# Rotating queries and keys: a shuffle on VectorE, or two DMAs between even and odd partitions

## The chip, the core and the metric

The kernel runs on one core of one Trainium2 chip. The metric is the device time of one execution in microseconds (us). Of the kernel before, three runs are at hand, with the median 1198.29 us (1196.13 to 1202.39), and one execution with a profile. The core has five engines that each work through their own list of instructions in order: TensorE (PE in the profile; its weight loads, PEld, are shown apart), VectorE (DVE), ScalarE (ACT), GpSimd (POOL) and SyncE (SP), which here only issues DMAs. ACT and POOL can issue DMAs too.

## What is computed

The input x holds 8 sequences of 512 tokens with 512 features. After a LayerNorm, a branch of linear attention (s) and a mixture of experts (g) are multiplied and added to x:

```python
xn = _layernorm(x)
q = silu((xn @ Wq).reshape(b, n, 16, 32));  k = silu((xn @ Wk).reshape(b, n, 16, 32))
q = _lrpe_rotate(q);  k = _lrpe_rotate(k)
o = _lightning_attn(q, k, v, log_lam)      # chunks of 128 tokens, decay by head
s = _gated_group_rmsnorm(o, xn @ Wg1 @ Wg2, norm_weight) @ Wo
g = silu(moe(xn))                          # top 4 of 16 experts, and a shared one
out = x + s * g

def _lrpe_rotate(x):                       # the last axis is one head, d = 32
    x1, x2 = x[..., :16], x[..., 16:]
    return concatenate([x1 * cos - x2 * sin, x1 * sin + x2 * cos], axis=-1)
```

So a feature i of a head, below 16, is rotated together with feature i + 16 of the same head, by an angle that depends on i and on the token. Scores are products of a rotated query with a rotated key over the 32 features of a head; they don't change if the features of both are put in another order.

## The kernel before, in words

Queries and keys are held with features on the partitions and the 512 tokens of a sequence along the free axis. The 16 heads lie in 4 groups (g) of 4 heads, so a group fills the 128 partitions, 32 for each head. Everything is float32. The weights and tables are prepared on the host (from L1310 on) and in `shape_constants`.

The work has four stages (times from the profiled execution):

1. 0 to about 200 us: norm, transpose, routing and the shared expert of all 8 sequences, with the attention of sequence 0 woven in.
2. About 200 to 330 us: the attention of sequence 1, beside the table of which token goes to which expert, and the first loads of expert weights (768 KB each).
3. About 330 to 735 us: 136 blocks of 128 tokens through their experts (gather on POOL, transpose by DMA, two matrix products).
4. About 735 to 1192 us: the attention of sequences 2 to 7, woven with `mixture`, which fetches for each tile of 128 tokens the rows m (shared expert, L1194) and s (attention of sequences 0 and 1, L1198) through SP and four rows yg of the experts (L1203) by indirect DMAs of POOL, adds them up on POOL and DVE, and multiplies and adds into xo (x itself, loaded at L1229; DVE at L1240, POOL at L1244, stored at L1245).

`rotated` makes one group of keys or queries. Four matmuls (L627, each in the profile's count two: four steps over the 512 features of the input, float32) put it into a PSUM bank; ACT takes it out with a silu into s (L632); DVE makes w_ from s by a `stream_shuffle` that exchanges the halves of 16 in each block of 32 partitions (L634, the list SWAP); then DVE multiplies s with the cosines into r (L636), w_ with the signed sines (L637), and adds (L638). s and w_ are taken from a ring of four buffers ("tmp"), which the attention's other short-lived tiles share (g1, rs, so). r is kT or qT of the group, two buffers each.

Who needs them: `by_token` transposes kT on PE (L654) and DVE multiplies it with the decay of its chunk (kd, L657); `scores` forms states from kd and v (L674), multiplies kT with qT in 4 banks (ps, L685), and DVE makes the scan of the states (L689), qd from qT (L705) and sc from ps with the decay mask (L711, four for a group). `output` (L722, L733) adds up po from both, and DVE multiplies it with the gate (L737). At the end of a sequence come the norm (`squares`, `normed`, L764, L769) and the projection with Wo (pw, L776).

The order on PE is written out by hand: `enter` (for sequence 2) begins with key 0, query 0, key 1, the transposes of key 0, query 1; `sequence` then takes for each group g its scores, key g+2, the transposes of group g+1, query g+2, and the output of group g, with projections of the sequence before between; groups 0 and 1 of the next sequence are made at its end. `last_sequence` does the same for sequence 7. Calls of `step` move the mixture of other tiles on. PSUM banks are scarce: four with the tag "a" (scores and others), one "k" (the transposes and states), one "m" (pk of `rotated`), two "d" (pq, po, pw). On the other engines a scheduler fixes the order, from each instruction's place in the program and the marks `behind(engine)`. SP issues all loads and stores except two loads of expert weights, which ACT issues (L1040), and the gathers, which POOL issues.

Of the kernel before, what the change touches and what calls it, by code (L numbers as in the profile page):

```python
# [20 lines left out]
B, N, D = 8, 512, 512  # L21
H, HD = 16, 32
G, HG = 4, 4
# [22 lines left out]
GROUP = 16  # L46


SWAP = [(i + HD // 2) % HD for i in range(HD)]


def shape_constants():

    f = np.float32
    c = {}
    lam = -(f(2.0) ** (f(-8.0) * (np.arange(H, dtype=f) + f(1.0)) / f(H))).astype(f)
    i = np.arange(C, dtype=f)
    diff = i[None, :] - i[:, None]
    dec = np.exp(lam[None, :, None] * np.maximum(diff, f(0.0))[:, None, :])
    c["dmask"] = np.where(diff[:, None, :] >= 0, dec, f(0.0))  # L60
    dq = np.exp(lam[:, None] * (i[None, :] + f(1.0)))
    c["dq"] = np.repeat(dq.reshape(G, HG, 1, C), HD, axis=2).reshape(G, P, C).transpose(1, 0, 2)
    c["dk"] = np.exp(lam[None, :] * (f(C) - f(1.0) - i[:, None]))
    lc = np.exp(lam * f(C))
    c["lamc"] = np.repeat(lc.reshape(G, HG, 1), HD, axis=2).reshape(G, P).T

    c["carry"] = np.tile(c["lamc"][:, :, None, None] * (np.arange(NC - 1) > 0), (1, 1, HD, 1))
    half = HD // 2
    theta = (f(BASE) ** (f(-2.0) * np.arange(half, dtype=f) / f(HD))).astype(f)
    ang = (np.arange(N, dtype=f)[None, :] * theta[:, None]).astype(f)  # L70
    c["cos"] = np.tile(np.cos(ang), (2 * HG, 1))
    c["sin"] = np.tile(np.concatenate([-np.sin(ang), np.sin(ang)], axis=0), (HG, 1))
    c["ident"] = np.eye(P)


    sel = np.zeros((P, H - HG + Q))
    exp = np.zeros((H, G, P))
    for g in range(G):
        for j in range(HG):
            sel[j * HD : (j + 1) * HD, H - HG + j] = 1.0 / HD  # L80
            exp[g * HG + j, g, j * HD : (j + 1) * HD] = 1.0
    c["sel"] = sel

    c["tri"] = np.triu(np.ones((P, P)), 1)
    c["iota_e"] = np.tile(np.arange(E), (P, 1))
    c["reset"] = np.tile((np.arange(NT) > 0)[None], (P, E)).reshape(P, E * NT)
    out = {k: np.ascontiguousarray(v.reshape(P, -1), dtype=f) for k, v in c.items()}
    out["exp"] = exp.reshape(H, D).astype(f)
    out["iota_b"] = (np.arange(P, dtype=f)[:, None] // Q * NBQ + np.arange(NBQ, dtype=f)).astype(f)
    out["token"] = (  # L90
        np.arange(NT)[None, :] * P + np.arange(P)[:, None] - B * N // 2).astype(np.float32)
    return out
# [3 lines left out]
def tile_block(ctx: ExitStack, tc: tile.TileContext, a: dict, out: bass.AP):  # L96
    nc = tc.nc
    PSUM = bass.MemoryType.PSUM
    x = a["x"]
# [5 lines left out]
    def bank(tag, name):  # L105
        return pp.tile([P, 512], F32, tag=tag, name=name, bufs={"a": 4, "k": 1, "m": 1, "d": 2}[tag])
# [10 lines left out]
    def load(pool, name, shape, dt=F32):  # L117
        t = pool.tile(shape, dt, tag=name, name=name, bufs=1)
        flat = t if len(shape) == 2 else t.rearrange(
            "p a b -> p (a b)" if len(shape) == 3 else "p a b c -> p (a b c)")  # L120
        nc.sync.dma_start(flat, a[name])
        return t

    def load_w(pool, name):
        t = pool.tile([P, KC, D], F32, tag=name, name=name, bufs=1)
        nc.sync.dma_start(t, a[name].rearrange("(k p) n -> p k n", p=P))
        return t
# [40 lines left out]
    wv = load_w(const, "wv")  # L168
# [6 lines left out]
    wk = load_w(const, "wk")  # L175
    cos = load(const, "cos", [P, N])
    sin = load(const, "sin", [P, N])
    wq = load_w(const, "wq")
# [23 lines left out]
    @contextmanager  # L202
    def on_pe():

        with tc.issue_after(last_pe[-1]) if last_pe else nullcontext():
            yield
        traced = nc.cur_bb.bb.instructions
        last_pe.append(next(
            i for i in reversed(traced) if i.engine == mybir.EngineType.PE))
# [413 lines left out]
    def rotated(b, g, n, w):  # L623
        ps = bank("m" if n == "k" else "d", f"p{n}_{b}_{g}")
        for k in range(KC):
            with on_pe():
                nc.tensor.matmul(  # L627
                    ps, lhsT=w[:, k, g * P : (g + 1) * P], rhs=xT_of[b][:, k, :],
                    start=(k == 0), stop=(k == KC - 1))
            between[0]()  # L630
        s = att.tile([P, N], F32, tag="tmp", name=f"s{n}_{b}_{g}", bufs=TMP)
        nc.scalar.activation(s, ps, AF.Silu)  # L632
        w_ = att.tile([P, N], F32, tag="tmp", name=f"sw{n}_{b}_{g}", bufs=TMP)
        nc.vector.stream_shuffle(w_, s, SWAP)  # L634
        r = att.tile([P, N], F32, tag=f"{n}T", name=f"{n}T_{b}_{g}", bufs=2)
        nc.vector.tensor_tensor(r, s, cos, ALU.mult)  # L636
        nc.vector.tensor_tensor(w_, w_, sin, ALU.mult)  # L637
        nc.vector.tensor_tensor(r, r, w_, ALU.add)  # L638
        return r

    def key(b, g):
        kT_of[g] = rotated(b, g, "k", wk)

    def query(b, g):
        qT_of[g] = rotated(b, g, "q", wq)
# [705 lines left out]
```

## Time and profile before

| | |
|---|---|
| median of three runs | 1198.29 us |
| the profiled execution | 1193.77 us |
| its span in the profile | 1191.9 us |
| mean granted TensorE clock | 0.991 |
| ACT busy | 459.7 us (39%), 934 instructions |
| POOL busy | 452.2 us (38%), 432 instructions |
| DMA, mean | 182 GB/s, 217.42 MB |
| the cos-multiply of L636, kT and qT | 732 and 869 ns |
| the sin-multiply of L637, swk and swq | 814 and 725 ns |
| the addition of L638, kT and qT | 772 and 945 ns |
| the silu of L632, sk and sq | 598 and 600 ns |
| the shuffle's list (L634 LOAD_MASK_SELECT) | some 10 ns |

The profile gives for each group of instructions the line of the code, the engine, the operation, the tile written and the tile read, the shape, the count, the busy time, the mean of one in ns, and the idle time of the engine just before them with what released it. "pk<-xT,wk" is a matmul that writes pk. The span is 1.9 us shorter than the execution's time. [...] An entry with SPq is the issue of a DMA on SP's queue, and its length is that of issuing, not of the transfer.

### The profile page before, as it was taken

To read this page: it belongs to the slowest core of one execution; us is meant where nothing else is said; L and a number is where in the kernel's file an instruction comes from. 1 tells how busy PE (TensorE), PEld (TensorE's weight loads), DVE (VectorE), ACT (ScalarE), POOL (GpSimd) and SP (SyncE) were. 2 spreads that over 40 slices of the span, in tenths; PEclk is the share of its full clock that TensorE was granted. 3 is DMA by queue.
4 is the path that set the end of the run, shared out by engine and by line. 5 is a ranking of instruction groups with operands and counts; after the bars stand their busy time and mean duration, and the time that the engine had idled before them with its cause. 6 is when DMAs were issued, how large, how long until landed. Compare 5 with 4: busy or idle time off the path is not lost. (4 is left out here: it accounts for less than half of the span.)

```text
span 1191.9 us, 21613 instructions
## 1 busy us (share of the span) xinstructions
PE 1145.7 (96%) x7780; PEld 700.9 (59%) x7780; DVE 722.8 (61%) x1557; ACT 459.7 (39%) x934; POOL 452.2 (38%) x432
## 2 busy tenths in 40 slices
PE   7999999989999999999999999999999989999997
PEld 3445554456577777677777775555554645545553
DVE  6356754889124444344444444969979598698684
ACT  4444454144374444444444442251251422422531
POOL 3211203200213333233333331762886848858211
PEclk9998999989999999999999999999999999999999
DMA  9964341191659999899999895931845637534112
GB/s 340 327 236 173 120 168 44 41 377 38 183 160 224 226 227 221 217 232 232 221 227 229 229 226 181 336 120 51 277 133 184 200 95 235 163 115 144 36 35 73
DMA packets 163499, 217.42 MB, mean 182 GB/s; under 512 B 89536, under 2 KB 98880, under 8 KB 161472
## 3 DMA queue, kind: packets, MB, share of 16 engines
q1 hardware_dynamic: 141984, 144.10, 40.5%
q0 software_dynamic: 21120, 70.34, 21.4%
q8 instruction: 65, 1.06, 0.4%
q10 hardware_dynamic: 288, 1.57, 0.4%
q14 instruction: 42, 0.34, 0.1%
HBM read 125.71 MB, written 72.42 MB: 166 GB/s over the span
## 5 line engine op out<-in xcount | busy, mean ns | idle before, releaser
L1103 PE MATMUL pgu<-wexp,xt 128*128 x1088 | 257.8, 380 | 3.2 <-ACT xt L1084 2.7
L1103 PEld LDWEIGHTS pgu<-wexp,xt 128*128 128x128 f32 x1088 | 205.8, 190 | 90.9 <-issue 39.2
L1062 POOL DMA_INDIRECT xg<-xn_d,slot x79 | 75.1, 951 | 243.4 <-DVE y L1133 159.2
L1108 DVE TENSOR_TENSOR slb<-slb,pgu 128x128 f32<-128x128 f32 x136 | 39.2, 288 | 196.7 <-ACT slb L1107 142.0
L1203 POOL DMA_INDIRECT yg<-y_d,place x128 | 143.0, 1117 | 34.6 <-issue 18.6
L1086 ACT COPY xt<-pl 128x512 uint16<-128x512 uint16 x136 | 104.3, 767 | 134.1 <-DMA pl<-xg 77.5
L1124 PE MATMUL py<-wexp,hT 128*128 x272 | 139.3, 594 | 0.1
L583 PE MATMUL pv<-wv,xT 128*128 128x512 f32 x256 | 119.4, 602 | 3.5 <-ACT sh L372 2.3
L627 PE MATMUL pk<-xT,wk 128*128 128x512 f32 x256 | 118.2, 603 | 1.7 <-DVEq L1167 1.7
L627 PE MATMUL pq<-xT,wq 128*128 128x512 f32 x256 | 117.3, 599 | 0.0
L776 PE MATMUL pw<-wo,on 128*128 128x512 f32 x224 | 103.8, 612 | 5.8 <-DVE m L1240 5.2
L1244 POOL TENSOR_TENSOR xo<-xo,m 128x512 f32<-128x512 f32 x31 | 45.1, 1454 | 141.3 <-DVE m L1240 133.4
L1062 POOL DMA_INDIRECT more<-xn_d,slot x57 | 54.0, 947 | 109.9 <-DVE y L1133 109.0
L711 DVE TENSOR_TENSOR sc<-ps,dmask 128x512 f32<-128x512 f32 x128 | 79.5, 680 | 5.6 <-remote 3.8
L627 PEld LDWEIGHTS pq<-xT,wq 128*128 128x128 f32 x256 | 47.8, 193 | 52.8 <-issue 51.3
L627 PEld LDWEIGHTS pk<-xT,wk 128*128 128x128 f32 x256 | 46.1, 190 | 52.0 <-issue 49.6
L1133 DVE TENSOR_SCALAR y<-py,xg 128x512 f32<-128x512 f32 x79 | 59.3, 750 | 28.2 <-PE py L1124 27.7
L776 PEld LDWEIGHTS pw<-wo,on 128*128 128x128 f32 x224 | 42.5, 196 | 56.9 <-issue 47.8
L583 PEld LDWEIGHTS pv<-wv,xT 128*128 128x128 f32 x256 | 45.7, 191 | 49.6 <-issue 43.5
L1107 ACT ACTIVATE slb<-pgu 128x128 f32<-128x128 f32 x136 | 37.8, 278 | 87.5 <-PE pgu L1103 83.1
L694 ACT COPY blocked<-state 32x96 f32<-32x96 f32 x96 | 30.7, 320 | 81.6 <-DVE state L689 68.8
L1133 DVE TENSOR_SCALAR y<-py,more 128x512 f32<-128x512 f32 x57 | 42.7, 750 | 19.7 <-PE py L1124 19.6
(172 smaller groups left out, 1761.5 us busy)
## 6 DMA issues: line engine op xcount, KB each, us to landing
y_d<-y SPq DMA_DIRECT2D x136, 256.0 KB
wexp<-in_experts SPq DMA_DIRECT2D x14, 768.0 KB
sh_d<-sh SPq DMA_DIRECT2D x32, 256.0 KB
m<-sh_d SPq DMA_DIRECT2D x32, 256.0 KB
xo<-in_x SPq DMA_DIRECT2D x32, 256.0 KB
out<-xo SPq DMA_DIRECT2D x31, 256.0 KB
x<-in_x SPq DMA_DIRECT2D x7, 1024.0 KB
xT_d<-xT SPq DMA_DIRECT2D x7, 1024.0 KB
```

Of the source, the lines that this page charges most:

```text
L583: nc.tensor.matmul(pv, lhsT=xT_of[b][:, k, t * P : (t + 1) * P], rhs=wv[:, k, :], start=(k == 0), stop=(k == KC - 1))
L627: nc.tensor.matmul(ps, lhsT=w[:, k, g * P : (g + 1) * P], rhs=xT_of[b][:, k, :], start=(k == 0), stop=(k == KC - 1))
L711: nc.vector.tensor_tensor(s, pss[j].rearrange("p (c t) -> p c t", t=C), dmask[:, g * HG + j].unsqueeze(1).to_broadcast([P, NC, C]), ALU.mult)
L776: nc.tensor.matmul(pw, lhsT=on_of[b][:, g, t * P : (t + 1) * P], rhs=wo[:, g, :], start=(g == 0), stop=(g == G - 1))
L1062: nc.gpsimd.indirect_dma_start(out=row(i), out_offset=None, in_=xn_d, in_offset=bass.IndirectOffsetOnAxis(ap=slot[:, i : i + 1], axis=0))
L1086: nc.scalar.copy(xt[:, KP:, :].bitcast(U16).rearrange("p k (t h) -> p h k t", h=2), turned(i).rearrange("p (h k) t -> p h k t", h=2))
L1103: nc.tensor.matmul(pg[:, : 2 * F], lhsT=xt[:, k, :], rhs=wflat[:, bass.ds(off + k * 2 * F, 2 * F)], start=(k == 0), stop=(k == KC - 1))
L1108: nc.vector.tensor_tensor(sl, sl, pg[:, F : 2 * F], ALU.mult)
L1124: nc.tensor.matmul(py, lhsT=hT_of.pop(i), rhs=wflat[:, bass.ds(off_of.pop(i) + KC * 2 * F, D)], start=True, stop=True)
L1133: gone.append(nc.vector.tensor_scalar(y, py, row(i).bitcast(F32)[:, bass.ds(at, 1)], None, ALU.mult).ins)
L1203: nc.gpsimd.indirect_dma_start(out=yg, out_offset=None, in_=y_d, in_offset=bass.IndirectOffsetOnAxis(ap=place[:, r, g : g + 1], axis=0))
L1244: nc.gpsimd.tensor_tensor(xo, xo, m, ALU.add)
```

## The change

Two things are done, in three places.

The order of the features within a head is changed from 0, 1, …, 31 to 0, 16, 1, 17, …, 15, 31, so that the two features which are rotated into each other lie on neighbouring partitions, an even one and the odd one behind it. The host reorders the columns of Wq and Wk (`paired`), and the tables of cosines and signed sines follow the same order. V, the gate and Wo keep theirs. Shapes don't change.

The shuffle on DVE is replaced by two DMAs that ACT issues right behind its silu: one writes the odd partitions of s to the even partitions of w_ (64 partitions of 512 float32, 128 KB), the other the even ones to the odd ones. The three DVE operations that follow are as before.

```diff
-SWAP = [(i + HD // 2) % HD for i in range(HD)]
...
-    c["cos"] = np.tile(np.cos(ang), (2 * HG, 1))
-    c["sin"] = np.tile(np.concatenate([-np.sin(ang), np.sin(ang)], axis=0), (HG, 1))
+    c["cos"] = np.tile(np.repeat(np.cos(ang), 2, axis=0), (HG, 1))
+    c["sin"] = np.tile(np.stack([-np.sin(ang), np.sin(ang)], axis=1).reshape(HD, N), (HG, 1))
...
         w_ = att.tile([P, N], F32, tag="tmp", name=f"sw{n}_{b}_{g}", bufs=TMP)
-        nc.vector.stream_shuffle(w_, s, SWAP)
+        pairs, of_pairs = (
+            t.rearrange("(p two) n -> p two n", two=2) for t in (w_, s))
+        for i in range(2):
+            nc.scalar.dma_start(pairs[:, i, :], of_pairs[:, 1 - i, :])
         r = att.tile([P, N], F32, tag=f"{n}T", name=f"{n}T_{b}_{g}", bufs=2)
...
+    def paired(w):
+        return arr(w).reshape(D, H, 2, HD // 2).swapaxes(2, 3).reshape(D, D)
+
     given = {
-        "x": arr(L0_attn_x), "wq": arr(L0_attn_Wq), "wk": arr(L0_attn_Wk), "wv": arr(L0_attn_Wv),
+        "x": arr(L0_attn_x), "wq": paired(L0_attn_Wq), "wk": paired(L0_attn_Wk),
+        "wv": arr(L0_attn_Wv),
```

There are 64 rotations (8 sequences, 4 groups, keys and queries), so 64 shuffles go and 128 DMAs come. In the profile of the changed kernel the lines ahead of the rotation have numbers lower by three; from L635 on they are the same.

## The prediction

> **What bounds the kernel now.** I read the page's busy table first, then the busy times by stage, the groups by shape, the waits, and last the timeline around single rotations.
>
> ```profile
> PE 1145.7 (96%) x7780; PEld 700.9 (59%) x7780; DVE 722.8 (61%) x1557; ACT 459.7 (39%) x934; POOL 452.2 (38%) x432
> ```
>
> TensorE is the bound: 1145.7 of 1191.9 us, so 46 us of idle are all that any change on other engines can win. The rotations touch VectorE (DVE), ScalarE (ACT) and the DMA engines, so their share of those 46 us counts. By stage (columns: stretch, length, busy of PE, PEld, DVE, ACT, POOL, PE clock, DMA share, GB/s):
>
> ```profile
> 200.00:330.00 130.00, 123.72 (x1046) 70.21 (x1044) 86.73 (x175) 47.94 (x108) 19.74 (x17) 0.96 0.47 154
> 330.00:735.00 405.00, 400.74 (x1794) 296.60 (x1792) 167.78 (x408) 179.40 (x418) 122.95 (x131) 1.00 0.89 218
> 735.00:800.00 65.00, 61.64 (x582) 35.19 (x583) 48.02 (x79) 19.50 (x41) 46.24 (x41) 1.00 0.68 236
> 800.00:1110.00 310.00, 301.82 (x2577) 164.18 (x2576) 249.86 (x387) 99.38 (x192) 213.99 (x175) 0.99 0.50 157
> ```
>
> Rotations lie everywhere but in the experts (330 to 735): 8 in 0–200, 8 in 200–330, 48 behind 735. Where sequences 2 to 7 run, DVE is 75 to 80% busy: it is near PE, not ahead of it. The waits (waiter, releaser: us, count, longest):
>
> ```profile
> DVE swk L634 <- ACT sk L632: 21.1, 8, 5.2
> DVE swq L634 <- ACT sq L632: 9.4, 10, 2.0
> PE pw L776 <- DVE m L1240: 5.2, 3, 2.9
> PE p L613 <- DVE sc L711: 2.2, 1, 2.2
> ```
>
> The idle stretches of PE in the timeline that DVE ends add up to some 15 us (2.8 in the routing, 5.4 in sequence 1, 5.2 at 902, 982 and 1062 in the last stage, the rest below 1 each). At 18 rotations DVE was already waiting for the silu; elsewhere it arrives up to 4.3 us late.
>
> **What is removed.** 64 shuffles:
>
> ```profile
> L634 DVE STREAM_SHUFFLE swq<-sq 128x512 f32<-128x512 f32 x32 | 23.3, 727 | 0.0
> L634 DVE STREAM_SHUFFLE swk<-sk 128x512 f32<-128x512 f32 x32 | 23.3, 727 | 0.0
> ```
>
> Busy 46.6 us; start to start one takes 0.62 (740.05 to 740.67 below), so DVE is given 64 × 0.62 = 40 us. On PE's path lies only what is inside the 15 us. The 5.2 us at 902, 982 and 1062 have DVE backlogged for over 10 us ahead of them, with two to four shuffles in each backlog: 1.2 to 2.5 us each, so at most 5 us; I take 4.
>
> **What is added.** Two exchanges of 64 partitions × 2 KB (128 KB each) per rotation, 128 issues on ACT's queue, 16.8 MB, against 217 MB moved now. No such transfer is in the trace. Nearest rows: a 128 KB store of normed rows issued at 146.65 landed 1.71 us later, and 256 KB in a quieter part of the last stage:
>
> ```profile
> 827.91 0.34 SPq L1245 DMA_DIRECT2D out<-xo  x1
> 828.34 0.38 SPq L1194 DMA_DIRECT2D m<-sh_d  x1
> 830.00 0.33 SPq L1229 DMA_DIRECT2D xo<-in_x  x1
> ```
>
> The load at 830.00 needs the buffer that the store of 827.91 reads, so that landed within 2.09. Silu end to both halves landed is then 0.1 for the handover, 0.33 for the first issue, 1.71 for the second: 2.15 if the halves overlap. The Trainium skill (DMA: Bandwidth & Descriptors, Rules for kernel authors) speaks against this change: two transfers to disjoint partition halves serialize, since both spread over the same 16 engines, and one transfer of 128 partitions is to be used. The rows make the second 128 KB worth 2.09 − 1.71 = 0.38, so 2.5 serialized. [...] I take 2.5 where DMA is quiet[...]. The loads of the mixed stages land later (2 to 5 us at 827–1010, 5.2 to 9.4 at 740–768), so 3 to 3.5 in the last stage, 4 to 5 where loads pile up. Below 2.15 I see no way; the upper bound is those 9.4.
>
> The cos-multiply (0.6) no longer waits for the shuffle, so the sin-multiply is late by R − 0.6 instead of 0.6: about 2 us later per rotation in the last stage. DVE runs in order: what is behind it waits too. What covers that is in the timeline (start, us):
>
> ```profile
> 739.21 3.60 PE L627 MATMUL pq<-xT,wq 128*128 128x512 f32 x8
> ...
> 739.41 0.60 ACT L632 ACTIVATE sk<-pk 128x512 f32<-128x512 f32 x1 [8.20 <-PE pk L627]
> ...
> 740.05 0.72 DVE L634 STREAM_SHUFFLE swk<-sk 128x512 f32<-128x512 f32 x1
> ...
> 740.67 0.67 DVE L636 TENSOR_TENSOR kT<-sk,cos 128x512 f32<-128x512 f32 x1
> 740.70 2.75 SPq L1194 DMA_DIRECT2D m<-sh_d  x5
> ...
> 742.84 0.60 ACT L632 ACTIVATE sq<-pq 128x512 f32<-128x512 f32 x1 [2.84 <-PE pq L627]
> ```
>
> kT of group 0 is done at 742.67 and PE transposes it at 746.08; qT is done at 746.10 and its scores begin at 750.26. So the matmuls of the next projection (3.6 us) cover 3.4 and 4.2 us; groups 2 and 3 have over 10. Two microseconds fit. In the changed program's order the waiting sin-multiply often has other DVE work put in front of it (kd and the addition of L1240 ahead of swk of group 2; three of the four norm multiplies around swq of group 0). In sequences 3 to 7 I therefore put the delay at nothing, with bounds −6 (all relief) and +8 (some 20 sin-multiplies with 0.4 us each reaching PE); with the relief: −4.
>
> **Where the cover is gone.** Three places.
>
> First, the start of the last stage. In the built program the DMAs of SP's and ACT's queues share eight completion semaphores in turn, and a DMA waits until the one before it on its semaphore has landed. At most rotations that DMA landed long before the silu ends. In sequence 2 it hadn't: against the silu's end, the awaited loads of m, s and xo landed +4.5 and +6.1 us late (query 0: 743.44 against 747.98 and 749.52), +6.4 (key 1), +6.2 and +7.6 (query 1), +3.3 and +6.5 (key 2), +2.8 (query 2). So qT of group 0 is done at about 749.5 + 2.5 to 4 + 1.3 = 753.5 and not 746.1; scores of group 0 move from 750.3 to about 754, with DVE held in front of qd, the next key and sc; by the second place po of group 0 moves from 758.7 to some 764. ACT stands still as well, with the silu of the next projection behind the exchange, and SP's next loads stand behind exchanges in turn. From then on loads are done and nothing adds. Loss 7 us (3 to 9).
>
> Second, sequence 1 (200–330): DVE 67% busy, its sc already ends 3.2 us of PE's idle, and the sin-multiplies are in front of the sc multiplies; the expert weights (768 KB each, landing 4 to 17 us after issue) fill the engines. 8 rotations by half a microsecond: 4 (1 to 8).
>
> Third, sequence 0 inside the norm and routing: two issues (0.7, under load up to 1.4) stand on ACT ahead of evacuations that PE waits for (1.8 and 1.7 us already), and loads keep DMA at 0.98 in the first 60 us: 3 (0 to 7).
>
> The reordered tables and weight columns cost nothing: same shapes, same matmuls. The experts have no rotation: 0. POOL's gathers share the DMA engines with 16.8 MB more: at the 335 GB/s that the first 60 us moved, 50 us in 64 portions, in stages whose DMA share is mostly 0.1 to 0.7: 0, inside the bounds above.
>
> Sum: −4 + 7 + 4 + 3 = +10 us. The profiled execution took 1193.77, so 1204; the median of the runs is 1.0038 times that execution: 1208.
>
> **Rivals.**
> Relief decides (faster). 15 us of PE's idle end at DVE; if 40 us less DVE work takes 10 of it away and the exchanges stay hidden also in sequence 2 (the loads ahead land sooner than I map them), 1184 in the profile, 1188. For it: backlogs at 902, 982, 1062. Against: most of the 15 us are single events, in stages where the exchange is slowest.
> Everything hidden (no change): the gains and stage starts cancel, 1194 to 1197, about 1199. For it: 3.4 to 4.2 us of cover against 2. Against: sequence 2's semaphores.
> The in-order wait decides (far slower). If the exchange takes 4 us or more in the last stage too, as loads beside it do, the sin-multiply is 3.4 late and cover of 3.4 is used up: from there each further microsecond at groups 0 and 1 (4 rotations × 6 sequences) reaches PE. At 4.7: 24 × 0.8 = 19 more, so 1223, 1228. For it: loads of 2 to 5 us at 827–1010. Against: these are 256 KB behind others on their queue.
>
> **Chances.** Forecast 0.50, own range 1201 to 1216, median 1208; hidden 0.17 (1199); relief 0.13 (1188); in-order waits 0.20 (1216 to 1245, middle 1228). A difference under 0.5% (6 us) is about what a measurement of this kernel can't tell from none. Faster 0.13; same 0.17 and the lower sixth of the forecast, 0.25; slower 0.62. The range 1190 to 1230 leaves out about half of the relief case and half of the last.
>
> **What would show it.** In the changed profile: PE's idle ended by DVE at the scores of 750 to 766 (forecast 7 us) and none new behind 830; the wait of the sin-multiply on a DMA, 64 long, about 2 us each where DVE isn't backlogged; DVE busy near 676; the gaps at 902, 982 and 1062 down from 5.2 to 1 or 2. I am wrong if the exchanges in quiet stretches take over 4 us, if PE's new idle lies in sequences 3 to 7, or if ACT waits for other queues' transfers anywhere else than in sequence 2.

## The result, and the profile after

The changed kernel takes 1248.43 us (median of four runs, 1248.09 to 1253.02); the kernel before took 1197.21 beside it. The ratio is 1.0444, with the 95% interval 1.0416 to 1.0472: slower by some 53 us, outside the range that was given. The profiled execution took 1248.1 us, its span is 1246.3 us, 54.4 more than before.

The busy table first:

```profile
PE 1164.2 (93%) x7780; PEld 708.6 (57%) x7780; DVE 686.6 (55%) x1429; ACT 457.9 (37%) x932; POOL 448.5 (36%) x432
```

DVE lost its 64 shuffles and 36 us of work. TensorE has the same 7780 matmuls, but is idle for 82.1 us and not 46.2 (36 more), and is busy for 18.5 us longer with the same work. Most of the second part is the clock: its mean over the span fell from 0.991 to 0.979, and 0.021 of 1246.3 us against 0.009 of 1191.9 us makes some 15 us (an estimate from these four figures).

The stages (same columns as before; the stretches are the same in time, and from 735 on the later kernel has got less far in them):

```profile
200.00:330.00 130.00, 113.47 (x1008) 65.36 (x1010) 81.14 (x155) 47.79 (x106) 16.56 (x12) 0.92 0.38 138
330.00:735.00 405.00, 401.32 (x1786) 293.90 (x1781) 162.25 (x394) 176.70 (x410) 128.17 (x135) 1.00 0.92 223
735.00:800.00 65.00, 52.71 (x283) 29.23 (x282) 29.26 (x52) 11.16 (x27) 35.05 (x33) 0.95 0.76 263
800.00:1110.00 310.00, 286.13 (x2430) 155.14 (x2429) 211.46 (x297) 94.19 (x181) 176.70 (x149) 0.97 0.53 165
```

The experts are untouched. Where rotations are, PE's busy time and its clock (the third column from the end) fell together. Taken at the start of the first silu of each sequence, the delay against the kernel before grows like this (from the two traces; the last column is a second profiled execution of the changed kernel on another chip, e9 below). On that chip the kernel before takes 1186.35 us, 7 less than its execution traced here, so the last column shows less than was lost there:

| up to key 0 of | before, us | after, us | later by | later by, in e9 |
|---|---|---|---|---|
| sequence 1 | 210.7 | 214.2 | 3.5 | 5.1 |
| sequence 2 | 739.4 | 755.2 | 15.8 | 13.9 |
| sequence 3 | 803.2 | 832.6 | 29.4 | 24.5 |
| sequence 4 | 878.1 | 921.4 | 43.3 | 28.1 |
| sequence 5 | 956.6 | 1007.8 | 51.2 | 31.5 |
| sequence 7 | 1115.0 | 1167.7 | 52.7 | 30.2 |

What the engines wait for now:

```profile
DVE swq L637 <- DMA swq<-sq: 61.9, 19, 7.6
...
DVE swk L637 <- DMA swk<-sk: 31.2, 13, 7.4
...
PE pk L654 <- DVE state L689: 18.8, 6, 5.8
...
PE pn L538 <- DVE sc L711: 9.5, 2, 6.7
...
PE ps L685 <- DVE kT L636: 5.8, 1, 5.8
...
PE p L610 <- DVE sc L711: 3.8, 1, 3.8
PE pk L654 <- DVE kT L638: 3.7, 2, 3.1
```

DVE stands still for 93 us at 32 sin-multiplies, up to 7.6 us at one. PE does not name the exchange anywhere. It waits for a scan of states (15.6 of the 18.8 us at the last query of sequences 3 to 5) and, in sequence 1, for sc (the 9.5 us of pn): work that stands behind a sin-multiply on DVE. The 3.8 us of p, also in sequence 1, stand behind DVE's work on the table of tokens, and were 2.2 in the kernel before. At two places, both in group 0 of sequence 2, it waits for the rotated product itself: 3.1 us for the key, and 5.8 us for the query. The view puts the 5.8 down to a cos-multiply that was over at 774.64; the addition of the query ended last, at 775.24:

```profile
773.35 0.69 DVE L637 TENSOR_TENSOR swq<-swq,sin 128x512 f32<-128x512 f32 x1 [7.02 <-DMA swq<-sq]
...
774.56 0.68 DVE L638 TENSOR_TENSOR qT<-qT,swq 128x512 f32<-128x512 f32 x1
```

```profile
775.30 2.09 PE L685 MATMUL ps<-qT,kT 32*128 32x128 f32 x32 [5.80 <-DVE kT L636]
```

One place shows whole how the wait reaches PE through other work. DVE in the middle of sequence 3 (an instruction can start a little before the time shown of the one before is over: the sin-multiply at 886.90 runs to 887.59, and qd starts at 887.51):

```profile
877.60 2.17 DVE L636 TENSOR_TENSOR qT<-sq,cos 128x512 f32<-128x512 f32 x1
886.90 0.69 DVE L637 TENSOR_TENSOR swq<-swq,sin 128x512 f32<-128x512 f32 x1 [7.14 <-DMA swq<-sq]
887.51 0.55 DVE L705 TENSOR_TENSOR qd<-qT,dq 128x384 f32<-128x384 f32 x1
...
891.12 0.34 DVE L689 TENSOR_TENSOR_SCAN state<-carry,pk 128x96 f32<-128x96 f32 x1
```

This is the query of group 3, which nobody needs yet: its scores begin at 900.96, 26 us after the start of its silu (17 us in the kernel before). The scan at 891.12 belongs to group 2; PE had made its input by 880.4, and the transposes of the next keys go into the same PSUM bank, so they need the scan to be done. PE at the same time:

```profile
881.99 3.70 PE L580 MATMUL pv<-wv,xT 128*128 128x512 f32 x8
891.52 0.90 PE L654 MATMUL pk<-ident,kT 128*128 128x128 f32 x3 [5.83 <-DVE state L689]
892.22 6.07 PE L580 MATMUL pv<-wv,xT 128*128 128x512 f32 x8
```

Once the exchange has landed, DVE has 4.2 us of other work ahead of the scan (886.90 to 891.12). The stop costs 5.83 us, and then eight matmuls of pv take 6.07 us where the eight before them had taken 3.70. The busy times of 6 us each around it (PE, PEld, DVE, ACT, POOL, then the clock, DMA share and GB/s) say why:

```profile
880.00:886.00 6.00, 5.48 (x42) 2.88 (x42) 0.00 (x0) 0.00 (x0) 1.88 (x2) 1.00 1.00 356
886.00:892.00 6.00, 0.48 (x2) 0.48 (x3) 5.10 (x9) 0.49 (x2) 2.46 (x2) 0.86 0.54 180
892.00:898.00 6.00, 6.00 (x10) 2.63 (x10) 3.50 (x7) 1.89 (x5) 5.20 (x6) 0.57 0.77 238
```

From 880 to 886 DVE does nothing, though PE's results lie ready, while the DMA engines are full (1.00); from 892 to 898 PE is granted 0.57 of its clock. The chain of waits gives the transfer behind it (start, us, what):

```profile
874.34 4.26 DMA xo<-in_x
...
878.62 8.18 DMA swq<-sq
```

The second half of the exchange was issued only when a load of xo on SP's queue had landed, and then took 8.18 us.

By the trace's semaphore events, the time from the silu's end until both halves have landed is 2.6 us at 24 of the 64 rotations, where nothing else moves. The middle of all 64 is 4.0 us; 32 take over 4, and eight take 8 or more: both of group 2 in sequence 1 (8.0 and 11.4, beside expert weights), query 0, key 1 and query 1 of sequence 2 (8.6 to 14.0), the last query of sequences 3, 4 and 5 (11.5, 9.8 and 9.4). At six of these eight ACT had to wait for a semaphore before its first issue, 1.7 to 6.5 us.

### The profile page after: what moved, and what is told of

Read it like the earlier page. It is cut to its first block, busy times and chain, and to the rows that moved or that the text cites. A ratio compares the mean times of both kernels' runs of the same rounds, so it can differ in the third digit from the quotient of the medians.

```text
span 1246.3 us, 21675 instructions
## 1 busy us (share of the span) xinstructions
PE 1164.2 (93%) x7780; PEld 708.6 (57%) x7780; DVE 686.6 (55%) x1429; ACT 457.9 (37%) x932; POOL 448.5 (36%) x432
## 3 DMA queue, kind: packets, MB, share of 16 engines
q10 hardware_dynamic: 10528, 18.36, 4.0%
## 5 line engine op out<-in xcount | busy, mean ns | idle before, releaser
L580 PE MATMUL pv<-wv,xT 128*128 128x512 f32 x256 | 127.0, 634 | 3.8 <-ACT sh L369 2.4
L624 PE MATMUL pk<-xT,wk 128*128 128x512 f32 x256 | 122.0, 619 | 1.3 <-DVEq L1167 1.3
L1244 POOL TENSOR_TENSOR xo<-xo,m 128x512 f32<-128x512 f32 x31 | 41.9, 1352 | 177.5 <-DVE m L1240 150.4
L776 PE MATMUL pw<-wo,on 128*128 128x512 f32 x224 | 100.2, 594 | 0.6 <-DVE on L769 0.6
L580 PEld LDWEIGHTS pv<-wv,xT 128*128 128x128 f32 x256 | 48.7, 204 | 53.7 <-issue 47.6
L637 DVE TENSOR_TENSOR swq<-swq,sin 128x512 f32<-128x512 f32 x32 | 23.3, 729 | 66.7 <-DMA swq<-sq 61.9
```

The lines of the kernel that those rows point to most:

```text
L580: nc.tensor.matmul(pv, lhsT=xT_of[b][:, k, t * P : (t + 1) * P], rhs=wv[:, k, :], start=(k == 0), stop=(k == KC - 1))
L624: nc.tensor.matmul(ps, lhsT=w[:, k, g * P : (g + 1) * P], rhs=xT_of[b][:, k, :], start=(k == 0), stop=(k == KC - 1))
L776: nc.tensor.matmul(pw, lhsT=on_of[b][:, g, t * P : (t + 1) * P], rhs=wo[:, g, :], start=(g == 0), stop=(g == G - 1))
L1244: nc.gpsimd.tensor_tensor(xo, xo, m, ALU.add)
```

## The experiments

Theory A: the time is lost because DVE, which works in order, stands at the sin-multiply until a late exchange has landed, with state, qd and sc of other groups behind it; PE stops for these, and its clock falls after each stop. Rivals: B, the 128 issues on ACT, their semaphores and their bytes cost it, whoever reads them; C, the new order of the features; D, not what lies beside the exchanges but the shared semaphores and their own length make them late; E, PE itself waits for late keys and queries, as at the two places in sequence 2. Chips differ in the time of the kernel before (1184 to 1197 us), so ratios to it, measured on the same chip, are compared; expectations of e1 to e8 in us are meant with a kernel before of 1197 us.

**e1, the layout alone, and e2, no exchange at all.**

```diff
-        (two DMAs)
+        nc.vector.stream_shuffle(w_, s, [i ^ 1 for i in range(HD)])   # e1
...
-        nc.vector.tensor_tensor(w_, w_, sin, ALU.mult)
+        nc.vector.tensor_tensor(w_, s, sin, ALU.mult)                 # e2, with the DMAs deleted
```

> The new feature order alone: the shuffle stays, with neighbours exchanged in place of halves, and no DMA. Theory A (VectorE stands at the sin-multiply until an exchange of 4 to 14 us has landed, and TensorE's clock falls in the idle time that follows) and theory B (the 128 issues and their transfers themselves hold ACT, SP's loads and the DMA engines, whoever reads them) both expect the time before, 1197 within 5 us. Theory C (the new order of weights and tables costs something) expects part of the 51 us, over 1210.

> Leaves the exchange out: the sin-multiply takes the silu's output itself. No shuffle and no DMA, so it shows what 64 shuffles less are worth by themselves. A and B expect 1190 to 1197 (relief of 0 to 7 us, the waits of PE on DVE at 902, 982 and 1062 gone); the rival of the prediction in which relief decides expects 1185 to 1189.

e2 leaves the exchange out. Measured: e1 1.0017 (0.9996 to 1.0038), e2 0.9992 (0.9965 to 1.0019). C falls. And the relief of DVE is worth between 4 us gained and 2 lost by e2: removing 40 us of DVE work and putting nothing in its place buys nothing that these runs can tell from zero.

**e3, the same DMAs, but nobody reads them.**

```diff
+        nc.vector.stream_shuffle(w_, s, [i ^ 1 for i in range(HD)])
+        idle = dram.tile([P, N], F32, name=f"id{n}_{b}_{g}", tag=f"id{n}_{b}_{g}")
...
-            nc.scalar.dma_start(pairs[:, i, :], of_pairs[:, 1 - i, :])     # pairs of w_
+            nc.scalar.dma_start(pairs[:, i, :], of_pairs[:, 1 - i, :])     # pairs of idle
```

> The shuffle feeds the rotation, and ACT issues the same two DMAs behind each silu all the same, 64 partitions of 2 KB each, but into a buffer in HBM that nobody reads. A expects 1198 to 1208: what is lost is the waiting of VectorE, and that is gone. B expects 1235 to 1250, since issues, semaphores and bytes are all there.

Measured 1.0024 (0.9992 to 1.0057). Its page, busy times and ACT's queue (packets, MB, share of the engines):

```profile
PE 1150.4 (96%) x7780; PEld 704.9 (59%) x7780; DVE 722.4 (60%) x1557; ACT 461.1 (38%) x934; POOL 449.6 (38%) x432
...
q10 hardware_dynamic: 10528, 18.36, 4.2%
```

The queue carries the same 18.36 MB as in the changed kernel, and the time is that of before. By the semaphore events the copies land as late as the exchanges (middle 3.9 us behind the silu, seven of 64 at 8 or more). B falls: issues, semaphores and bytes together cost under 0.6%. It is the reading that costs. (These copies go to HBM; unread copies within SBUF were not run.)

**e4, the shuffle back at 13 rotations, the eight latest among them.**

```diff
+        if b == 2 or (b == 1 and g == 2) or (2 < b < 6 and (n, g) == ("q", 3)):
+            nc.vector.stream_shuffle(w_, s, [i ^ 1 for i in range(HD)])
+        else:
             (two DMAs)
```

> The exchange by DMA stays at 51 of 64 rotations; the 13 whose exchange landed latest in the trace get the shuffle back (sequence 1: both of group 2; all 8 of sequence 2; the query of group 3 of sequences 3, 4 and 5). A expects 1193 to 1204, nearly all of the 51 us back or a little more. B expects 13/64 of it back, some 1238.

The 13 are not quite the latest: they hold the eight that took 8 us or more, and the other five of sequence 2 (3.4 to 6.9 us), while two of 6.6 and 6.7 us keep the exchange. Measured 1.0055 (1.0026 to 1.0085): some seven eighths of the loss is gone, though 51 of 64 exchanges remain. The longest wait of DVE at a swq falls from 7.6 to 5.7 us, and none of PE's stops behind 800 is over 2.2 us.

**e5, e7 and e8: three that did not do what they say.** e5 asks later for the 1 MB load of the transposed input, e7 puts every sin-multiply into the program one rotation late, e8 does both.

```diff
+            if g == 0 and b > FIRST:
+                load_xT(n)                   # e5, taken out of the loop over the sequences
...
+        settle()                             # e7: the sin-multiply and addition of the rotation before
+        unsettled.append(rest)
```

> The change as it is, but from sequence 3 on the load of the next sequence's transposed input (1 MB, nobody needs it for 80 us) is asked for behind the scores of group 0 of the sequence before, and no longer lands on top of the exchange for the last query of the sequence before that. Theory A with bulk loads as the cause of the late landings: the last query of sequences 3, 4 and 5 lands 4 to 6 us behind its silu and not 9 to 11.5, and 15 to 25 of the 51 us return: 1222 to 1235. Rival D (the waits come from the shared completion semaphores and from the exchange's own length, not from what lies beside it): no change, 1243 to 1250.

> The change as it is, but the sin-multiply and the addition of a rotation are put into the program behind the exchange and cos-multiply of the next one (the last query of a sequence behind the sc of group 2), so VectorE has other work in front of the wait. If the loss is VectorE's in-order wait holding up kd, state and sc of other groups (theory A): most returns, 1198 to 1215. If TensorE itself waits for late keys and queries (theory E): little, over 1230.

> Both of the last but one and the first of this call: sin-multiply one rotation behind, and the 1 MB load later. A expects 1195 to 1206, nothing to choose from the kernel before; E expects 1222 or more.

Measured 1.0386 (1.0314 to 1.0458), 1.0402 (1.0351 to 1.0452) and 1.0345 (1.0299 to 1.0392). The traces show that the scheduler undid the moves: in e5 the load was issued at the same place (875.62, 2.9 us behind the silu of the last query of sequence 3; in the changed kernel 2.7), and in e7 the sin-multiply of that query stood in front of qd and the scan as before; e8 shows both. So they decide nothing between A, D and E; e10 to e12 below force the order.

**e6, one DMA of 128 partitions.** It leaves the exchange out.

```diff
-            (two DMAs)
+        nc.scalar.dma_start(w_, s)
```

> Leaves the exchange out: one DMA of all 128 partitions copies the silu's output straight to w_, in place of two of 64. It asks what the pair costs over one transfer of 256 KB. Theory A: landing falls by the one issue, 2.6 to 2.1 us where quiet, and hardly where loads lie beside it: 1233 to 1245. If the two halves hinder each other, or their 64 more turns on the shared semaphores matter (theory D), more comes back: 1215 to 1230.

Measured 1.0301 (1.0233 to 1.0369). Where nothing else moves, w_ is there 2.26 us behind the silu's end and not 2.6; over sequences 3 to 7 the middle falls from 3.8 to 2.8. The surprise is the last query of sequences 3, 4 and 5, with 3.1, 2.7 and 2.3 us in place of 11.5, 9.8 and 9.4: ACT doesn't wait before these three issues, where it had waited 1.7 and 2.5 us at two. With half the DMAs the turns on the shared semaphores fall elsewhere, but the bytes in flight beside the copies differ too, so what spared them is not shown. The time itself, as a ratio, lies at the lower edge of what A expected (1233 to 1245 of 1197: 1.030 to 1.040) and above D's (1.015 to 1.027), with an interval that reaches into both. Against the change on another chip (e9, 1.0382) it is 10 us less, which the two intervals don't keep clear of nothing.

**e9, the change again; e10, only the last query held back; e11, all one rotation late, by force; e12, the big load behind the exchange.**

```diff
+        with behind(DVE):                          # e10: behind the sc of group 2, query of group 3 only
+            unsettled.pop()()
...
+            with behind(DVE):                      # e11: every rotation, behind the cos-multiply of the next
+                unsettled.pop(0)()
...
+                if g + 3 == G and b >= FIRST and b + 2 < B:        # e12
+                    with behind(ACT):
+                        load_xT(b + 2, nc.scalar)
```

> The change itself once more, as the yardstick for the other three on the same chip: 45 to 55 us over the kernel before.

> The change with one alteration of VectorE's order: in sequences 2 to 7 the sin-multiply and the addition of the last query (group 3) are held behind the state, qd and sc of group 2, for which TensorE is waiting; the exchange is issued as before and lands as late as before. Theory A (in-order wait of VectorE is what TensorE feels): TensorE's stops of 5 us at the transposes of sequences 3, 4 and 5 vanish, 18 to 27 of the 51 us return. Theory E (TensorE itself waits for the late query): nothing returns, within 5 us of the change.

> As e7, where the scheduler had moved the sin-multiply of the last query back to the front: now every sin-multiply is bound behind VectorE's last instruction at its place in the program, one rotation late. A expects 10 to 22 us over the kernel before (what stays is sequence 2, where exchanges land 9 to 14 us late, and sequence 1). E expects over 35.

> As e5, where the 1 MB load of the transposed input stayed at its place on SP's queue: now ACT issues it, right behind the two exchanges of the last query, from sequence 2 on, so that it can't be ahead of them. If the load beside it makes that exchange late (theory A): the last query of sequences 3, 4 and 5 lands within 5 us of its silu, and 15 to 27 of the 51 us return. If the shared semaphores and stores do it (theory D): lateness stays over 7, nothing returns.

| | ratio to before | interval |
|---|---|---|
| e9, the change | 1.0382 | 1.0329 to 1.0434 |
| e10 | 1.0267 | 1.0221 to 1.0312 |
| e11 | 1.0066 | 1.0046 to 1.0087 |
| e12 | 1.0283 | 1.0235 to 1.0330 |

e9 loses 44 us by its medians, the lower edge of what was expected. e11 decides. Its exchanges land as late as before: middle 4.0 us, 32 over 4 and 14.0 at the most, against 4.0, 32 and 13.9 in e9. Only DVE's order differs. Its waits:

```profile
PE ps L698 <- DVE qT L649: 9.8, 4, 6.1
...
DVE swk L648 <- DMA swk<-sk: 6.9, 4, 3.0
...
DVE swq L648 <- DMA swq<-sq: 4.9, 3, 3.1
```

DVE waits 11.8 us for exchanges where it had waited 88.8 in e9 (93 in the first profile), and of 45 us of loss (0.0382 × 1186) 37 are gone, more than A expected. A holds. E is left with the stops at group 0 of sequence 2, where the product itself is late: 6.06 us at the scores (the largest of the first line) and 2.4 at the transposes, much as in the change. A late exchange also holds its w_ in the ring of four buffers for longer; e11 holds it longer still, so that is not the loss. e10 alone, six queries moved, returns 14 us (0.0115 × 1186), less than the 18 expected. PE's waits for the scan fell from 14.6 us (4.6 at the most) in e9 to 5.7 (1.8), while in its one trace the two stops of sequence 2 were 3.8 us longer. e12 returns 12 us, also short of what was expected, and the lateness it should have cured stayed at two of three places (7.9, 10.4 and 4.3 us): so a load issued behind the exchange still makes it late, or the semaphores do; A's sub-claim that the big load must be ahead of it falls. Where the 12 us come from is not shown: the two profiled spans, 1222.1 and 1223.9, hardly differ.

**e13, the order of e11 with the shuffle; e14, e11 with the shuffle at 10 rotations.**

```diff
+        nc.vector.stream_shuffle(w_, s, [i ^ 1 for i in range(HD)])       # e13, everywhere
...
+        if b == 2 or (b == 1 and g == 2):                                 # e14, else two DMAs
```

> The order of e11 (each sin-multiply bound one rotation late) with the shuffle in place of the exchange. If e11's return comes from taking VectorE's waits away, the order by itself is worth nothing where there is nothing to wait for: within 5 us of the kernel before. If e11 was fast because the new order is better in itself, and hid a cost of the exchange: faster than before by over 8 us.

> e11 with the shuffle at the 10 rotations whose exchange lands over 8 us late behind expert weights or behind the first loads of m, s and xo (sequence 1 group 2, all of sequence 2). If e11's last 8 us are these landings reaching TensorE as data (stop of 6 us at the scores of sequence 2), they go: 0 to 6 us faster than before, the only version that could beat it. If they are the cost of 128 issues on ACT: still 6 to 8 us slower.

Measured e13 1.0028 (1.0006 to 1.0051), e14 0.9986 (0.9965 to 1.0008). The order gains nothing by itself (if anything it costs, with an interval of 1 to 6 us), so it hid no cost in e11. With the late rotations of sequences 1 and 2 shuffled, the last 8 us are gone too; with 54 rotations by DMA the kernel can't be told from the one before. No version beats the kernel before by more than the measurement.

## Why the prediction was wrong

It forecast slower, rightly, and +10 us where there were +51 to +53. The direction was no luck: sequences 0 to 2 lose, as it said, and by more. The size failed in sequences 3 to 7. By its steps:

- **Relief, −4.** e2 allows +2 to −4, so in the order of the change −4 is the most that it can be. In the order of e11, where DVE hardly waits, 54 shuffles fewer gave 5 us (e14 against e13, 1186.0 against 1190.96). The size is possible; in the change itself it is drowned. Its sign came: PE's three stops behind m, 5.2 us, are gone.
- **The exchange's length, 2.5 us where quiet.** Right: 2.6. The terms differ: an issue on ACT takes 0.47 to 0.61 us, not 0.33, and the halves land 1.92 and 2.07 us after their issue, not 1.71. The halves hardly hinder each other where it is quiet: the second takes 0.15 us longer from its issue than the first, where the sum had put 0.38 for serializing. The pair is whole 2.6 us behind the silu, one transfer of the same bytes 2.26. That one transfer is the better choice, as the Trainium skill advises (DMA: Bandwidth & Descriptors, Rules for kernel authors), is likely by e6 but not clear of its noise. The upper bound of 9.4 us was passed at five exchanges, up to 14.0; at all five ACT had first waited 1.7 to 6.5 us for its turn on a semaphore.
- **3 to 3.5 us in the last stage.** Too small: sequences 3 to 7 have a middle of 3.8, and 18 of 40 are over 4.
- **"Groups 2 and 3 have over 10 … In sequences 3 to 7 I therefore put the delay at nothing."** This is the step that failed. The slack was measured from the rotation to the matmul that reads its product. But the waiting instruction holds everything behind it on DVE, and the slack of that counts: at the last query, qd and the scan of group 2 are behind it, and PE needs the scan within 5 us of making its input. The trace of before has the same order in sequence 3, and shows the slack:

```profile
847.43 0.68 DVE L637 TENSOR_TENSOR swq<-swq,sin 128x512 f32<-128x512 f32 x1
...
852.88 0.34 DVE L689 TENSOR_TENSOR_SCAN state<-carry,pk 128x96 f32<-128x96 f32 x1
```

```profile
854.29 0.49 PE L654 MATMUL pk<-ident,kT 128*128 128x128 f32 x3
```

The query of group 3 is done at 850.2 and its scores begin at 861.75: the slack of over 10 that the prediction counted. The scan is done at 853.2 and the transposes begin at 854.3: the slack that decided, 1.1 us. In place of −4 these sequences gave +23 (29.4 to 52.7), and +6 in e9, whose column falls short. e10 returns 14 us by moving just these six queries. Two of the prediction's own signs of being wrong came true here: new idle time of PE in sequences 3 to 5, and ACT waiting before an issue outside sequence 2 (3.8 us in sequence 1, 1.7 and 2.5 at the last queries of 3 and 4).
- **Sequence 2, +7.** Right mechanism and place (the awaited loads of m, s and xo, query 0 landing 14.0 us after its silu), half the size: 13.6 (15.8 to 29.4), in e9 10.6. **Sequence 1, +4:** 12.3, in e9 8.8; the exchange beside weight loads took 8.0 and 11.4 us, one stop of PE there 6.7 us, and the sum had half a microsecond for each rotation. **Sequence 0, +3:** 3.5, in e9 5.1.
- **The clock was not in the sum.** Each stop was priced by its length. PE is busy for 18.5 us longer, of which the clock explains some 15. The Trainium skill (TensorE: Matmul & The Clock Gate, "Why this matters for your kernels") says to allow no idle gaps over some 3 us between bursts of matmuls, since the clock then falls to half; after the stop of 5.83 us the rows show a granted clock of 0.57 and 6.07 us in place of 3.70. By the row, that stop costs 5.8 + 2.4 us at the first eight matmuls alone. The 3 us are no sharp limit here: the last section has stops on either side of it that went the other way.
- **The rival that came true** is the third, the in-order wait, held at 0.20 with 1228 and a range up to 1245, a little under what came. Its point of decision was put at 3.4 us and at groups 0 and 1; it decided at other places, above all at a group whose own product nobody needs yet. (Its sum also takes 0.8 us a rotation where its own figures, 4.7 − 0.6 − 3.4, give 0.7: 17 us and not 19.)

Open: how much of an exchange's lateness is contention with loads and gathers, and how much the wait for a turn on the shared semaphores. e6 and e12 change both and separate neither. In e11, with the same lateness, all but some 8 us are gone.

## What to carry to other kernels

When a step on an in-order engine is replaced by a transfer, the engine's next instruction becomes a wait: ask not when the result is needed, but when everything behind the wait is needed, in the order that was built. Give the waiting instruction a place behind work that is ready (e11 did it by one rotation, and the same late transfers then cost 8 us and not 45), or don't replace a 0.6 us instruction on an engine that isn't the bound: taking 40 us off DVE was worth 0 to 5 us here. And price a stop of PE that lasts several microseconds with the slow matmuls behind it.

## What the runs showed of the hardware that was not expected

Two DMAs of 128 KB issued 0.5 us apart land 1.92 and 2.07 us after their issue where nothing else moves, and one of 256 KB in 2.24. By the first and the last, 128 KB more cost 0.32 us, and 1.6 of the 1.92 don't depend on the size (an estimate from these two). Beside loads the same 128 KB take up to 8.8 us.

No length of a stop decides by itself whether the clock falls. It fell after stops shorter than 3 us. In the kernel before:

```profile
982.74 5.37 PE L776 MATMUL pw<-wo,on 128*128 128x512 f32 x8 [2.90 <-DVE m L1240]
```

The granted clock over these 5.37 us is 0.68. The same eight matmuls of pw take 3.60 us elsewhere, so the stop of 2.90 us cost 1.8 us more than its length. In the same trace a stop of 2.21 us ended at 244.82, and the clock over 245 to 255 is 0.66. In e7 a stop of 2.46 us left it alone (the eight matmuls of pv take 3.60 us as usual), and in e9 one of 3.50 us did:

```profile
877.45 0.55 PE L666 MATMUL pk<-ident,kT 128*128 128x128 f32 x3 [2.46 <-DVE state L701]
877.83 3.60 PE L580 MATMUL pv<-wv,xT 128*128 128x512 f32 x8
```

```profile
883.24 0.55 PE L654 MATMUL pk<-ident,kT 128*128 128x128 f32 x3 [3.50 <-DVE state L689]
883.62 3.60 PE L580 MATMUL pv<-wv,xT 128*128 128x512 f32 x8
```

So theory A's clause that the clock falls after each stop is too strong: of stops near 3 us it follows some and not others, and what else decides is not shown.
